# An RWKV block and a gated feed-forward layer: two of seven gate and up products split once more, one block's weight sums kept in SBUF

## The chip, the cores and the metric

The kernel runs on one core of one Trainium2 chip. The metric is the device time of one launch in microseconds; the median of three runs of the kernel before is 1233.91 us (1233.78 to 1234.72). One further execution was taken with the hardware profiler, and the profile below is of that one.

## What is computed

The input is `x`, 2048 tokens by 512 channels, all in float32. `_layernorm` is a plain normalization over channels; `attn` is an RWKV layer at its first position; then a gated feed-forward layer follows.

```python
def attn(x):                       # RWKV time mix and channel mix
    h = layer_norm(x, ln1_g, ln1_b); hh = time_shift(h)
    k = (h * tm_mk + hh * (1 - tm_mk)) @ Wk.T      # v and r likewise
    wkv = ...                                      # elementwise, of k and v
    x = x + sigmoid(r) * wkv @ Wo.T
    h = layer_norm(x, ln2_g, ln2_b); hh = time_shift(h)
    kk = (h * cm_mk + hh * (1 - cm_mk)) @ Wkey.T   # 512 -> 2048
    kv = silu(kk) @ Wval.T                         # 2048 -> 512
    return x + sigmoid((h * cm_mr + hh * (1 - cm_mr)) @ Wcr.T) * kv

def ffn(h):
    gate, up = split(h @ w_gate_up.T, 2)           # 512 -> 2 x 2048
    return (silu(gate) * up) @ w_down.T            # 2048 -> 512

x = x + attn(_layernorm(x))
x = x + ffn(_layernorm(x))
```

## The kernel before

The 2048 tokens are worked in four blocks of 512 (`TB`), numbered 0 to 3 in the code and called block one to four here. Each 512x512 weight is cut into quarters of 256x256, and each product with it is done by Strassen's scheme in Winograd's form: seven products of quarters instead of eight. The operands of these seven are the quarters A11, A12, A22 and B11, B12, B21, B22, and sums of quarters: S1 to S4 of the weight, T1 to T4 of the activation (T3 takes the place of B12). The sums of the activations are made by VectorE in `sums_of`. The weights' sums are made once: `prepare` loads the four quarters of a weight into tiles of the pool `prep` (six tiles), makes S1 to S4 with four VectorE additions, and writes them to DRAM from GpSimd's queue. Afterwards `weight` loads a quarter or a sum, 256 KB, from DRAM into a ring of twelve tiles (`wring`) on SyncE's queue. The down products, 2048 to 512, go one Strassen level deeper on one side, with their own prepared sums (`"d"` and `"dd"`).

One gate or up unit (`unit`) is one 512x512 weight against one block's operand `zT`. Its seven products are `step1` to `step7`; each has four matmul calls of 128x128 against 256 columns. Three of them share PSUM contents: `step1`'s result is copied by ScalarE from the bank `z` into the accumulator `accv`, on which `step2` goes on; after `step5`, `z` is copied into `accx`, on which `step3` goes on. The last three products of a unit (`step7`, `step3`, `step4`) are held and popped between the first products of what comes next. `sink` receives each finished quarter: for a gate, ScalarE's Silu; for an up, VectorE's multiplication with the gate's quarter into the hidden tiles.

The order on TensorE, VectorE and ScalarE is that in which the Python program emits instructions. The program has its own planner. After each product `tick` adds `SHARE` (0.88) times the product's planned time (`STEP`, 1.72 us) to a balance, `slack`, from which the planned cost of VectorE's work is taken. While the balance is positive, `tick` emits work that is not tied to a product: first steps of weight preparation (`prep_one`), each of which needs one `credit`, then a queue of urgent steps (`hot`: sums of operands), then the `background` (norms, mixes). `credit[1]` is what one tick adds to the credit, at most 2.0 are kept, and `pause` is the number of ticks between the loads of a preparation and its first addition. `need` emits all that is left of a named piece of work, whatever the balance says.

The stages at the end are in this order: `ffn_gate(0, 0)`; then for each block b the gate and up units g = 0 to 3, the first gate of block b + 1, and the down products of block b. `ffn_in(b + 1)` is the last norm of the next block: it adds the residual and `x`, takes the moments, forms the reciprocal root with eleven small VectorE steps, scales on VectorE (`scaled`), transposes on TensorE and evacuates with ScalarE. It is pushed to the background in block b after the second up unit; the residual and `x` are loaded by `load_resid`.

The list `late` gives the order of preparations: first those of the value weights, then all eight gate and up weights, then those for the down products. They are worked off in the background from the first attention blocks on, and the last ones while block one's gate and up units run.

PSUM has eight banks: `accv`, `accx` and a pool `ps` of six.

Of the kernel before, what the change touches and what calls it, by code (L numbers as in the profile page):

```python
# [15 lines left out]
P = 128  # L16
# [5 lines left out]
EPS = 1e-5  # L22
WAIT = 5
LONG = 6
STEP = 1.72
SHARE = 0.88
WARM = 24
# [36 lines left out]
def rwkv_ffn_kernel(  # L64
# [20 lines left out]
    up = ctx.enter_context(tc.tile_pool(name="up", bufs=10))  # L85
    prep = ctx.enter_context(tc.tile_pool(name="prep", bufs=6))
    small = ctx.enter_context(tc.tile_pool(name="small", bufs=3))
    ps = ctx.enter_context(tc.tile_pool(name="ps", bufs=6, space=bass.MemoryType.PSUM))
    pv = ctx.enter_context(tc.tile_pool(name="pv", bufs=1, space=bass.MemoryType.PSUM))
    px = ctx.enter_context(tc.tile_pool(name="px", bufs=1, space=bass.MemoryType.PSUM))  # L90
    dram = ctx.enter_context(tc.tile_pool(name="dram", bufs=1, space=bass.MemoryType.DRAM))


# [16 lines left out]
        return tokp.tile([P, NT, H], F32, tag="tok", name=name)  # L110

    def bank():
        return ps.tile([P, 2, HB], F32, tag="ps", name="ps")

# [29 lines left out]
    def value_part(q, k):  # L146

        if q < 4:
            return wv[q, k].rearrange("p (g c) -> p g c", c=P)
        m, kk = divmod((0, 1, 3, 2)[k], 2)  # L150
        return vsum[q - 4][:, :, kk, m * P : (m + 1) * P]

    for q in (A11, A12, A22, S1, S2, S3, S4):
        sources["vv", q] = [value_part(q, k) for k in range(4)]
# [40 lines left out]
    def ring(src):  # L195
        t = wring.tile([P, 2, HB], F32, tag="w", name="w")
        nc.sync.dma_start(flat(t), src)
        return t

    def weight(n, q):  # L200
        if q >= 4:
            need_sums(n)
            return ring(sums[n][q - 4])
        return ring(sources[n][q])

    def down_weight(q, k):

# [10 lines left out]
    def value_weight(q, k):  # L218

        if k >= 4:  # L220
            need_sums(("vv", q))
            return ring(sums["vv", q][k - 4]).rearrange("p a (h c) -> p (a h) c", c=P)
        if q >= 4:
            for g in range(4):
                need_sums(WVAL + g)
        t = wring.tile([P, 2, HB], F32, tag="w", name="w")
        t = t.rearrange("p a (h c) -> p (a h) c", c=P)
        nc.sync.dma_start(t, value_part(q, k))
        return t

    def load_x(b, queues=None):
        t = tok_tile("x")
# [58 lines left out]
    preps = deque()  # L291
    credit = [0.0, 0.0]
    pause = [WAIT]

    def prep_one():
        item = preps[0]
        if item[1] > 0:
            return False
        try:
            if next(item[2]) is not None:  # L300
                item[1] = pause[0]
        except StopIteration:
            preps.popleft()
            finished.add(("sums", item[0]))
            if len(preps) > 1 and item[3] > 1:
                begin(preps[1])
            elif preps:
                begin(preps[0])
        return True
# [7 lines left out]
    def prepare_all(ns, own, depth):  # L317
        empty = not preps
        for n in ns:
            preps.append([n, 0, prepare(n, own), depth, False])  # L320
        if empty:
            for item in list(preps)[:depth]:
                begin(item)
# [58 lines left out]
    nc.vector.memset(warm, 0.0)  # L382
    nc.scalar.activation(warm, warm, AF.Exp)

    pt = ps.tile([P, 2, HB], F32, tag="ps", name="warm")
    for _ in range(WARM):
        nc.tensor.transpose(pt[:, 0, 0:P], ident, ident)

# [41 lines left out]
    def tt(out, a, b, op):  # L430
        nc.vector.tensor_tensor(out, a, b, op)  # L431
        cost(size(out))
# [140 lines left out]
    def release():  # L573
        while held:
            pop_held()
# [7 lines left out]
    def unit(weights, Bs, sink, by_token, done=None, free=None):  # L583
# [86 lines left out]
        for s in order:  # L670
            if s is None:
                pop_held()
            else:
                s()
                tick()
        held.extend(((STEP, step7), (STEP, step3), (STEP, step4)))

    def plain_unit(n, B, sink, by_token, done=None, free=None, halfway=None, hold=False):

# [451 lines left out]
    def ffn_in(b):  # L1131
        r, xr = loads.pop(b)
        for t in range(NT):
            tt(r[:, t, :], r[:, t, :], xr[:, t, :], ALU.add)
            yield
        rs[b] = r
        mv = small.tile([P, NT, 2], F32, tag="mv", name="mv")
        yield from moments(r, mv)
        var = small.tile([P, NT], F32, tag="var", name="var")
        ts(var, mv[:, :, 1], EPS, None, ALU.add)  # L1140
        rstd = small.tile([P, NT], F32, tag="rstd", name="rstd")
        yield from rsqrt(var, rstd, NT)
        z = tok_tile("z")
        yield from scaled(r, z, mv, rstd)
        m, B = op_tile("zT")
        ops[b, "z"] = B
        yield 1

        def evacuate(c, pt):
            k = c // 2  # L1150
            nc.scalar.copy(
                m[:, 2 * k : 2 * k + 2, c % 2, :], pt.rearrange("p (j t) -> p j t", j=2)
            )

        yield from transposed(z, evacuate)
        finished.add((b, "z"))
        yield 1
        yield from sums_of(B)

    gated = {}  # L1160

    def ffn_gate(b, g):
        s = gated[b, g] = {}

        tile_of = q_tile if g % 2 else u_tile

        def sink(i, j, c):
            t = tile_of("s")
            nc.scalar.activation(t, c, AF.Silu)
            s[i, j] = t  # L1170

        unit([WG + g], [Lazy((b, "z"))], sink, False)

    def ffn_up(b, g):
        s = gated.pop((b, g))
        hid = hidden.setdefault(b, {})

        def sink(i, j, c):
            q = (B11, B12, B21, B22)[2 * i + j]
            if q not in hid:  # L1180
                hid[q] = hidden_tile()
            tt(hid[q][:, g], c, s[i, j], ALU.mult)
            if g == 3:
                made.add((b, q))
                if q in (B11, B22):
                    quarter_sums(b, 0 if q == B11 else 1)

        unit(
            [WU + g],
            [Lazy((b, "z"))],  # L1190
            sink,
            False,
            lambda: hidden_done(b, g),
            op_done if g == 3 else None,
        )

    def hidden_done(b, g):
        hid = hidden[b]
# [35 lines left out]

    def last_room():
        middle.close()
        pools["q"] = ctx.enter_context(
            tc.tile_pool(name="fq", bufs=4, reuse_waits="tile")
        )

    def quarters(t):
        return {2 * k + m: t[:, :, k, m * P : (m + 1) * P] for k in range(2) for m in range(2)}
# [212 lines left out]

    early = [WV, WCR, WO] + [WKEY + g for g in range(4)] + [WVAL, WVAL + 1]
    late = [("vv", q) for q in (A11, S4, S2, A12, S1, S3, A22)]
    late += [n + g for g in range(4) for n in (WG, WU)] + [("dd", A11)]
    late += [("d", k) for k in range(4)] + [("dd", q) for q in (S4, S2, A12, S1, S3, A22)]

    ctx.enter_context(
        tc.manual_schedule(
# [25 lines left out]
    for b in range(NB):  # L1488
        nxt = b + 2 < NB
        if nxt:  # L1490
            xin[b + 2] = load_x(b + 2)
        if b == NB - 1:
            load_resid(0)
        if b >= DEEP:
            credit[1], pause[0] = 1.0, LONG
        gate_unit(b)
        if b + 1 < NB:
            out_unit(b + 1)
        if b == DEEP:
            need((b, "ck"))  # L1500
            mixes.close()
            deep_room()
        need((b, "ck"))
        if nxt:
            push(f"norm{b + 2}", time_norm(b + 2))
        for g in range(4):
            up_unit(b, g)
            if b == 1 and g == 0:
                credit[1] = 0.55
            if b == NB - 1 and g == 0:  # L1510
                push((0, "z", "t"), ffn_in(0), op_free)
            if g == 0:
                if nxt:
                    push_mix(b + 2, "k", time_mix(b + 2, "k"))
                    push_residual(b + 2)
                    push_mix(b + 2, "r", time_mix(b + 2, "r"))
                if b + 1 < NB:
                    push(f"normb{b + 1}", channel_norm(b + 1))
                if nxt:
                    push_mix(b + 2, "v", time_mix(b + 2, "v"))  # L1520
                if b + 1 < NB:
                    push_mix(b + 1, "cr", channel_mix(b + 1, "cr"))
                    push_mix(b + 1, "ck", channel_mix(b + 1, "ck"))
        if b == 1:
            credit[1] = 0.8
        if b >= DEEP:
            credit[1] = 0.0
        down_unit(b)
        if nxt:
            for n, u in (("k", k_unit), ("r", r_unit), ("v", v_unit)):  # L1530
                u(b + 2)
    credit[1] = 0.75
    need((0, "z"))
    ffn_gate(0, 0)
    last_room()
    for b in range(NB):
        for g in range(4):
            if g > 0:
                need((b, "z"))
                ffn_gate(b, g)  # L1540
            if g == 0 and b + 1 < NB:
                load_resid(b + 1)
            ffn_up(b, g)
            if g == 1 and b + 1 < NB:
                push((b + 1, "z", "t"), ffn_in(b + 1), op_free)
        if b + 1 < NB:
            need((b + 1, "z"))
            ffn_gate(b + 1, 0)
        ffn_down(b)
    release()  # L1550
    flush()

# [77 lines left out]
```

## Time and profile before

| what | value |
|---|---|
| median of three runs | 1233.91 us |
| the profiled execution | 1231.09 us |
| its span, first to last instruction | 1229.0 us |
| TensorE busy | 1219.5 us, 6860 matmul records |
| VectorE busy | 780.3 us |
| ScalarE busy | 368.4 us |
| GpSimd busy | 186.6 us |
| DMA | 319.03 MB, mean 260 GB/s |
| granted TensorE clock | 1.000 |

Stages of the end, as the timeline shows them (from the span's start): block one's gate and up units from about 655 us to 752, the first gate of block two to 765, block one's down products to 809, then blocks two, three and four in the same way to 1229.

A line of the profile's groups names line, engine, operation, written and read tiles, shapes and count, then busy time and mean duration of one. The chain of waits starts at the last instruction and goes back, at each step to what released it. In the slices, each digit is the busy share of a fortieth of the span in tenths. A matmul call on float32 appears as two records, each with its own weight load. Matmuls overlap, so the spacing of starts, not the duration of one, is what a stream of them costs.

### The profile page before, as it was taken

How to read it: one execution, taken by the hardware profiler on the slowest of the kernel's cores; microseconds unless marked ns; L12 is line 12 of the kernel's file. 1: busy time of each engine (PE TensorE's matmuls, PEld its weight loads, DVE VectorE, ACT ScalarE, POOL GpSimd, SP SyncE). 2: the span in 40 equal slices, each digit the busy share in tenths (PEclk: the TensorE clock that was granted, in tenths of full speed). 3: DMA queues.
4: the chain of work that ended last, by engine and by line, in shares of the span. 5: the costliest groups of instructions: out<-in, count | busy, mean ns of one | idle time of the engine just before them, and what ended most of it. 6: DMA issues, size and time to landing. Idle time of an engine off the chain costs nothing.

```text
span 1229.0 us, 19201 instructions
## 1 busy us (share of the span) xinstructions
PE 1219.5 (99%) x6860; PEld 1106.3 (90%) x6860; DVE 780.3 (63%) x1451; ACT 368.4 (30%) x713; POOL 186.6 (15%) x334
## 2 busy tenths in 40 slices
PE   9999999999999999999999999999999999999998
PEld 8888888888888888998899888998899888998898
DVE  5877686577685666886775577646546364553466
ACT  5534252242532333323412222112221232112211
POOL 2232221223212222002201222200000000000000
PEclk9999999999999999999999999999999999999999
DMA  5768985899888988899889978995469745785576
GB/s 196 250 221 282 319 299 206 302 320 302 277 262 270 312 288 263 261 297 381 280 281 329 335 232 279 362 343 154 146 194 309 258 143 153 250 290 154 153 225 204
DMA packets 159620, 319.03 MB, mean 260 GB/s; under 512 B 19096, under 2 KB 32552, under 8 KB 158248
## 3 DMA queue, kind: packets, MB, share of 16 engines
q1 hardware_dynamic: 132000, 230.22, 58.4%
q0 software_dynamic: 25920, 84.96, 19.0%
q10 hardware_dynamic: 1608, 2.65, 0.7%
q8 instruction: 55, 0.90, 0.3%
q14 instruction: 37, 0.30, 0.1%
HBM read 268.46 MB, written 49.29 MB: 259 GB/s over the span
## 4 chain that ended last, share of the span: by engine, by line
PE 90%; DVE 4%; DMA 3%; ACT 2%; issue 1%; POOL 1%; ACTq 0%; DVEq 0%; POOLq 0%
PE ps L602 45%; PE ps L1342 21%; PE accx L602 9%; PE accv L602 9%; PE ps L704 5%; DMA raw<-in_w 2%; PE ps L487 1%; DMA vsum<-raw 1%; DMA row<-stats 1%; ACT mix L540 1%; DVE raw L431 0%; DVE e L439 0%; DVE h L435 0%; DVE st L445 0%; POOL raw L181 0%
## 5 line engine op out<-in xcount | busy, mean ns | idle before, releaser
L602 PE MATMUL ps<-zT,w 128*128 128x256 f32 x1280 | 289.3, 380 | 0.0
L602 PEld LDWEIGHTS ps<-zT,w 128*128 128x128 f32 x1280 | 242.4, 191 | 31.5
L602 PE MATMUL ps<-mix,w 128*128 128x256 f32 x920 | 211.1, 380 | 1.3 <-ACT u L633 1.3
L602 PEld LDWEIGHTS ps<-mix,w 128*128 128x128 f32 x920 | 174.3, 190 | 24.5 <-ACT u L633 1.7
L1342 PE MATMUL ps<-w,hid 128*128 128x128 f32 x1248 | 156.8, 275 | 0.0
L1342 PEld LDWEIGHTS ps<-w,hid 128*128 128x128 f32 x1248 | 149.7, 192 | 1.2
L1342 PE MATMUL ps<-w,quads 128*128 128x128 f32 x1056 | 133.5, 276 | 0.4 <-ACT r L1354 0.4
L1342 PEld LDWEIGHTS ps<-w,quads 128*128 128x128 f32 x1056 | 126.4, 192 | 1.1 <-ACT r L1354 0.5
L1354 ACT COPY r<-ps 128x128 f32<-128x128 f32 x168 | 44.5, 265 | 204.5 <-PE ps L1342 201.9
L431 DVE TENSOR_TENSOR raw<-raw 128x512 f32<-128x512 f32 x120 | 82.5, 688 | 30.9 <-issue 11.1
L431 DVE TENSOR_TENSOR u<-u,accx 128x512 f32<-128x512 f32 x64 | 43.8, 685 | 85.7 <-ACT accx L637 85.7
L431 DVE TENSOR_TENSOR hid<-hid 128x512 f32<-128x512 f32 x126 | 84.9, 687 | 2.0 <-ACT hid L1068 0.3
L622 ACT COPY accv<-ps 128x512 f32<-128x512 f32 x64 | 36.5, 571 | 158.0 <-PE ps L602 155.2
L637 ACT COPY accx<-ps 128x512 f32<-128x512 f32 x64 | 36.5, 570 | 132.7 <-PE ps L602 126.2
L431 DVE TENSOR_TENSOR u<-ps,u 128x512 f32<-128x512 f32 x64 | 44.2, 690 | 44.5 <-PE ps L602 40.6
L704 PE MATMUL ps<-mix,w 128*128 128x256 f32 x320 | 70.8, 380 | 1.1 <-DVE mix L439 1.1
L633 ACT COPY u<-ps 128x512 f32<-128x512 f32 x64 | 37.4, 584 | 109.5 <-PE ps L602 109.5
L704 PEld LDWEIGHTS ps<-mix,w 128*128 128x128 f32 x320 | 60.4, 191 | 9.5 <-DVE mix L439 1.8
L431 DVE TENSOR_TENSOR r<-ps,r 128x256 f32<-128x256 f32 x83 | 29.8, 359 | 51.5 <-PE ps L1342 47.1
L602 PE MATMUL accv<-zT,w 128*128 128x256 f32 x256 | 60.6, 380 | 0.0
L602 PE MATMUL accx<-zT,w 128*128 128x256 f32 x256 | 60.5, 380 | 0.0
L602 PE MATMUL ps<-w,t 128*128 128x256 f32 x264 | 59.4, 379 | 0.0
(179 smaller groups left out, 1593.7 us busy)
## 6 DMA issues: line engine op xcount, KB each, us to landing
w<-sum SPq DMA_DIRECT2D x248, 256.0 KB, 4.2
w<-in_w SPq DMA_DIRECT2D x230, 256.0 KB, 4.2
w<-dd SPq DMA_DIRECT2D x112, 256.0 KB, 3.8
w<-vsum SPq DMA_DIRECT2D x56, 256.0 KB, 4.4
w<-vv SPq DMA_DIRECT2D x56, 256.0 KB, 4.0
raw<-in_w POOLq DMA_DIRECT2D x48, 256.0 KB, 6.7
w<-d SPq DMA_DIRECT2D x48, 256.0 KB, 3.5
sum<-raw POOLq DMA_DIRECT2D x40, 256.0 KB, 4.1
```

Of the source, the lines that this page charges most:

```text
L431: nc.vector.tensor_tensor(out, a, b, op)
L487: nc.tensor.transpose(flat[:, t * P : (t + 1) * P], h[:, t, c * P : (c + 1) * P], ident)
L540: nc.scalar.activation(dst(c), hT[:, c, 0:TB].rearrange("p (j t) -> p j t", j=2), AF.Copy, scale=onem[:, row - MK, c : c + 1],)
L602: mm = nc.tensor.matmul(pz[:, m, :], lhsT=lhsT, rhs=rhs, start=first and g == 0 and m == 0 and k == 0, stop=g == last and k == 1, skip_gro ...
L622: "z", A11, B11, True, pop_held, read=lambda: nc.scalar.copy(accv, acc["z"])
L633: nc.scalar.copy(tmp["u2"], acc["z"])
L637: nc.scalar.copy(accx, acc["z"])
L704: mm = nc.tensor.matmul(acc[i, j][:, m, :], lhsT=act[:, k, lo] if by_token else wg[:, k, lo], rhs=wg[:, k, :] if by_token else act[:, k, : ...
L1342: mm = nc.tensor.matmul(dst, lhsT=x[k][:, g, :], rhs=wt[:, g, :], start=first and g == 0, stop=g == 3, skip_group_check=True,)
L1354: nc.scalar.copy(st["r"][:, m, n * P : (n + 1) * P], st["z"])
```

## The change

Four things change, and the constants of the planner with them.

1. From the first up unit of block two on, gate and up units are done by `paired_unit`. It makes five products at full size. The two others, A11 with B11 and S3 with T3, are made for both at once by `inner`, one Strassen level deeper: seven products of half size, two calls each against 128 columns. These small steps belong to the next unit and are spread between the full products of the current one. The results lie in SBUF, in halves of one permanent tile (`pair`). A11's result is copied into `z` and `accv` by ScalarE, S3's (`plus`) is added by VectorE when (1, 1) and (1, 0) are formed. The first up unit of block two still makes all seven at full size, since no small steps precede it. One product of a unit is held instead of three.

2. The small products need the small sums of A11 and S3 of each weight (`small_sums`, eight VectorE instructions of 128 columns) and of the activation (`inner_sums`). For seven of the eight gate and up weights the sums are no longer prepared in the background: `jit_load` brings the quarters into the weight ring during block one, `jit_sums` makes S1 to S4 there, block one's units use these tiles directly, and they are written to DRAM for the later blocks. The list `late` loses these seven. All other preparations are emitted before block one's units begin.

3. PSUM is divided anew after block one's down products (`pair_room`, which first emits all held products): `accv`, `accx`, `z`, `w` and four banks of `ps`.

4. `ffn_in` scales on ScalarE, with the shift made from mean and reciprocal root first. It and the loads of its operands are queued earlier.

```diff
 def weight(n, q):
+    if n in jit and (n, q) not in at_once:
+        at_once.add((n, q))
+        while q not in jit[n]:
+            run_one(True)
+        return jit[n][q]
...
+def jit_load(n):
+    jit[n] = {}
+    for q in (A22, A21, A11, A12):
+        t = wring.tile([P, 2, HB], F32, tag="w", name="w")
+        nc.sync.dma_start(t, w[n, q])
+        jit[n][q] = t
+
+def jit_sums(n):
+    x = jit[n]
+    for o, i0, i1, op in ((S1, A21, A22, ALU.add), (S2, S1, A11, ALU.subtract),
+                          (S3, A11, A21, ALU.subtract), (S4, A12, S2, ALU.subtract)):
+        t = x[A21] if o == S3 else prep.tile([P, 2, HB], F32, tag="raw", name="raw")
+        tt(t, x[i0], x[i1], op)
+        x[o] = t
+        nc.gpsimd.dma_start(sums[n][o - S1], flat(t))
+        yield
+    for q in (A11, S3):
+        yield from small_sums(n, q, x[q])
...
 def prep_one():
...
+        item[5] += 1
+        if item[5] == AHEAD[0] and item[3] == 1 and len(preps) > 1:
+            begin(preps[1])
...
+def inner(n, b):                       # the small steps of one unit
+    def one():
+        st["w"] = [weight(n, A11), weight(n, S3)]
+        st["s"] = [inner_weight(n, A11), inner_weight(n, S3)]
+        mm(st["z"], A11, B11, True);  keep(0, 0)     # keep: ScalarE copy to SBUF
+        mm(st["y"][:, :, 0, :], A12, B21, True)
+    def two():    mm(st["z"], S2, T2, False);  keep(1, 0)
+    def three():  mm(st["z"], S1, T1, False);  keep(0, 1);  mm(st["y"][:, :, 1, :], S4, B22, False)
+    def four():   mm(st["z"], S3, "T3", False);  keep(1, 1)
+    def five():   mm(st["z"], A22, T4, False);  tt(r1, st["z"], r1, ALU.add)
...
+def paired_unit(at, b, n, after, sink, done=None, free=None):
+    small(); pop_held()
+    small(); product(z, S2, T2);      nc.scalar.copy(aw, z);    tick(); pop_held()
+    small(); product(accv, A12, B21); sink(0, 0, accv);         tick()
+    small(); product(z, S1, T1);      nc.scalar.copy(accx, z);  sink(1, 1, z, plus);  tick()
+    small(); nc.scalar.copy(z, r);    nc.scalar.copy(accv, r)
+    product(aw, A22, T4);             sink(1, 0, aw, plus);     tick()
+    held.append((STEP, last))         # last: product(accx, S4, B22); sink(0, 1, accx)
...
 def ffn_in(b):
-    yield from scaled(r, z, mv, rstd)
+    stt(shift, mv[:, :, 0], -1.0, rstd, ALU.mult, ALU.mult)
+    for t in range(NT):
+        nc.scalar.activation(z[:, t, :], r[:, t, :], AF.Identity,
+                             bias=shift[:, t : t + 1], scale=rstd[:, t : t + 1])
+        spent[0] += 0.3
+        yield
...
-late += [n + g for g in range(4) for n in (WG, WU)] + [("dd", A11)]
-late += [("d", k) for k in range(4)] + [("dd", q) for q in (S4, S2, A12, S1, S3, A22)]
+late += [WG, ("dd", A11)]
+late += [("d", k) for k in range(4)] + [("dd", q) for q in (A12, S4, S2, S1, S3, A22)]
...
-            credit[1], pause[0] = 1.0, LONG
+            credit[1], pause[0], AHEAD[0] = CREDIT, LONG, 2      # CREDIT = 0.65
...
-    credit[1] = 0.75
     need((0, "z"))
+    while preps:
+        need_sums(preps[-1][0])
     ffn_gate(0, 0)
...
+            if g == 1 and b == 0:
+                push((b + 1, "z", "t"), ffn_in(b + 1), op_free)
-            if g == 0 and b + 1 < NB:
+            if g == 0 and 0 < b < NB - 1:
                 load_resid(b + 1)
             ffn_up(b, g)
+            if g == 0 and b == 0:
+                load_resid(b + 1)
-            if g == 1 and b + 1 < NB:
+            if g == 0 and 0 < b < NB - 1:
                 push((b + 1, "z", "t"), ffn_in(b + 1), op_free)
...
         ffn_down(b)
+        if b == 0:
+            pair_room()
```

## The prediction, made before the result

> **What bounds the kernel now.** First the page's head and its slices: which engine is full, and is its clock whole.
>
> ```profile
> PE 1219.5 (99%) x6860; PEld 1106.3 (90%) x6860; DVE 780.3 (63%) x1451; ACT 368.4 (30%) x713; POOL 186.6 (15%) x334
> ...
> DVE  5877686577685666886775577646546364553466
> ...
> PEclk9999999999999999999999999999999999999999
> ```
>
> TensorE is busy 99% at a full granted clock; no other engine is above 63%. A busy PE row could still hide bad spacing, so next comes the chain that ended last, from 740 us on, where nearly all that the change touches lies.
>
> ```profile
> 770.23 39.30 PE ps L1342 x352
> 826.95 6.91 PE ps L602 x32
> 851.12 6.91 PE ps L602 x32
> ```
>
> The chain is PE instructions end to end. It also prices them: 39.30 / 352 = 0.1117 us for one record with 128 moving columns (down product), 6.91 / 32 = 0.2159 us for one with 256 (gate and up units). A matmul call leaves two records, so a product of four calls is 8 records, 1.73 us. Only products that vanish, or waits that appear, move the end. Third, the windows: block one's gate and up stage, then block two's.
>
> ```profile
> 655.00:752.00 97.00, 97.00 (x467) 85.99 (x466) 58.31 (x105) 25.19 (x45) 21.63 (x41) 1.00 0.87 295
> 809.00:895.00 86.00, 86.00 (x417) 76.33 (x417) 42.58 (x80) 21.70 (x40) 1.43 (x2) 1.00 0.61 191
> ```
>
> After the length the columns are PE, PEld, DVE, ACT, POOL, clock, DMA share, GB/s. DVE has 39 us free of 97 in block one, 43 of 86 in block two; DMA has room too. Last, what a wait costs when nothing lies between a product and the product that needs its copy:
>
> ```profile
> 1221.54 1.95 PE L1342 MATMUL ps<-w,hid 128*128 128x128 f32 x16
> 1223.84 1.16 PE L1342 MATMUL ps<-w,quads 128*128 128x128 f32 x8 [0.35 <-ACT r L1354]
> ```
>
> Sixteen records take 1.79 us, so the next should have started at 1223.33; it started 0.51 us late. That is the price of one product, ScalarE copy, product in a row.
>
> **The gain: two products split.** `paired_unit` does five of a unit's seven products at full size. The other two (A11 with B11, S3 with T3: 16 records of 256 columns) become seven products of half size for both at once in `inner`: 14 calls, 28 records of 128 columns. Before: 16 x 0.2159 = 3.455 us. After: 28 x 0.1117 = 3.126 us. Saved: 0.329 us a unit, since one level of Strassen saves an eighth. Units that get it: the first gate of block two stays `unit`, its up partner does all seven at full size, so 6 units of block two and 8 each of blocks three and four: 22. 22 x 0.329 = 7.2 us. All of it is on the path. The small steps stand between full products, 1.73 us apart, so their copies (0.27 us for 128 columns, 0.57 for 512) have time.
>
> The Trainium skill ("TensorE: Matmul & The Clock Gate", section "Back-to-back issue gap") gives about 81 ns per matmul at 128 columns in a stream of loads and matmuls; by it the saving would be 22 x (3.455 - 28 x 0.081), some 26 us, an estimate. Its section "LDWEIGHTS" speaks against halving columns: a weight load lasts columns of weight / 1.2, 107 ns, however few columns move; by that, an estimate of 10 us. The row's 0.1117 is close to the second, and the row decides.
>
> **What it adds on other engines, blocks two to four.** DVE: two 256-column adds and one of 512 per unit, 2 x 0.425 + 0.69 = 1.5 us; 4 small sums per block. The two accumulator updates of a unit (2 x 0.69) come back as the additions of `plus`. Eight units: +12 us, less 4 x 0.543 of the norm: about 53 of 84 us. ScalarE: four copies of 256 columns (0.27 to 0.57 each) and one of 512 more: about 2.1 us a unit, 40 of 84. Neither fills up. The tightest handoff is the single accumulator `z`: VectorE reads it, then ScalarE reloads it, before the next unit's S2 product. Between lie small step five (0.45), A22 (1.73), small one (0.89), the held S4 (1.73) and small two (0.45): 5.2 us against 0.69 + 0.60 + 0.57 of work. Cover 3.4 us; cost zero; without it the lag beyond 3.4 us per unit. Four `ps` banks in place of six: in the down stages VectorE frees a bank 0.3 to 1.1 us after its product and the next is due 2.7 us later: zero.
>
> SP: nine weight loads of 0.26 MB a unit instead of seven: seven in 12.1 us are 152 of the window's 191 GB/s, so nine make 191 + 2/7 x 152 = about 235, where other slices move up to 381. Four tiles of twelve are kept through a unit; eight still run ahead, about 8 x 1.7 us against 4.2 us to landing: zero. The residual loads move by one unit on the same queue behind loads that are twelve tiles ahead: zero.
>
> **What it adds on the path.** (a) `pair_room` calls `release` after the first down stage: the last two held products run back to back, each waiting for a copy: 2 x 0.51 = 1.0 us. Between 0.5 and 2 with a bank waited for. (b) The norm's scaling goes to ScalarE. The nearest row is a scale and shift there of the same shape (line 788), 803 ns, against 543 on VectorE: 4 x 0.80 = 3.2 us, charged 0.3 each by the planner, so often four in one tick. Queued behind them are the small steps' copies, wanted 1.2 us after a product (1.73 less 0.5). Bounds per block: 0 (spread over ticks) to 2.0 (all four ahead of one copy). With four banks, two held by `inner`, the four transposes and their 0.60 us evacuations may cost 0 to 0.8 more. For two paired blocks 0 to 5.6; I take 1.8, nearer the low end, because the trace shows such evacuations two to a tick and no PE gap. (c) Block one, below: 0.6.
>
> **Block one's weights in place.** Seven matrices leave the background (28 additions, between 388 and 505 us) and are summed inside block one: per unit four sums of 512 (0.69) and eight of 128 (0.294): 5.1 us of VectorE, plus 2.4 for the first. Leaving that window: 21 preparation sums (14.4 us) and four scalings (2.2). 58.3 - 14.4 + 35.5 + 2.4 - 2.2 = 79.6 of 97 us, 82%; the planner hands out up to 88%. Added wait: the fourth sum needs one of six `prep` tiles, and the earliest falls free when the unit's fourth product ends (6.9 us in); the planner reaches it after the second (3.5 us). Queued behind on VectorE: the up sinks and next block's norm. Five units x 3.4 = 17 us idle: 97 of 97. So cover is thin, though PE needs those results only about five products (8 us) later. If block two's norm is late at `need`, PE stands: bounds 0 to 7 (reciprocal root 2.4, four scalings 3.2, lag). I take 0.6, since before ended its norm at 727 us, 25 us early, and the change starts one unit earlier. POOL: six writes a unit at 0.55 = 3.3 us of 12.1, nothing waits.
>
> **Preparations pulled ahead.** All must be emitted before block one. In the third and fourth attention blocks' 77 ticks, 0.65 x 77 = 50 steps are allowed; about nine preparations x 5 = 45 are left. Before did 8.5 there. Short by one: four sums, 2.8 us on VectorE with its loads already landed, hidden by gate (0, 0). Cost 0; two short, up to 9.
>
> **Sum.** 1231.1 (the profiled execution; span 1229.0, 2.1 around it) - 7.2 + 1.0 + 1.8 + 0.6 = 1227.3. The median shown is 2.8 above that execution: 1230.1 us, 3.8 less than 1233.9. With nothing lost the floor is 1226.7. About 0.2% (2.5 us) is what a measurement of this kernel can tell from no change.
>
> **Rivals.** *Given back* (0.22): same mechanism, but (a) to (c) sum to 5 to 9: 1231.7 to 1236. For it: scalings at 0.80 charged 0.3, transposes with two free banks. Against: PE shows no such gap now, with ScalarE 30% busy. *VectorE becomes the bound in block one* (0.18), the slower side: the wait for `prep` tiles on top of 80 us. It decides once idle passes 17 us in the window; then block two's norm and sums end late and gate (1, 0) stands. Price: 3 us of overflow and the 7 of the norm's chain, up to 14 with the sums T1, T2 behind quarter sums: 1230.1 - 0.6 + 7 to 14 = 1237 to 1243. Against: the start one unit earlier. *The ring runs dry* (0.05): if a kept tile's slot is the one the next S4 load waits for, 4.2 - 2.6 = 1.6 us in each of 22 units, +35: about 1265. Against: slots are taken as they fall free. That the split does not happen is excluded by the code.
>
> **How the numbers follow.** Forecast 0.55: 1230.1, its own range 1227.2 to 1231.4. The range goes up into block one's case, to 1239; above it lie the ring and half of that case. Faster by over 0.2%: 0.55; within: the lower rival, 0.22; slower: 0.23.
>
> **What would show it.** Right: 616 records of 128 columns from the small steps at 0.11 each, gate and up units of blocks three and four about 11.8 us instead of 12.1, PE still 99%, VectorE near 80 of 97 in block one. Wrong: PE idle before a small step or before S2 released by ScalarE; a gap of microseconds at the first transposes of block two; PE waiting for `w` tiles.

## The result and the profile after

The changed kernel's median is 1245.99 us (1243.97 to 1250.42), beside 1234.32 (1233.78 to 1235.36) for the kernel before on the same chip: ratio 1.0098, 95% interval 1.007 to 1.0127. It is slower, by 11.7 us, where 3.8 us less were forecast; the time lies above the range, whose end was 1239.0. The profiled execution took 1246.27 us (span 1244.5), so by the two profiles the difference is larger, 15.2 us: the profiled execution of before was 3.2 us below its median here. What follows accounts for the two profiles.

First the head of the page after and its slices.

```profile
PE 1223.4 (98%) x7124; PEld 1110.5 (89%) x7124; DVE 819.9 (66%) x1582; ACT 419.4 (34%) x840; POOL 180.2 (14%) x322
...
PEclk9999999999999999999899999999999999999999
```

TensorE is busy 3.9 us longer than before, though its work is less, and one slice of the granted clock is an 8. Next the chain of waits and the windows that answer to those of before (block one's gate and up stage, then block two's paired units).

```profile
788.23 39.32 PE ps L1704 x352
921.04 1.73 PE accz L881 x8
```
```profile
664.00:761.00 97.00, 91.05 (x409) 78.58 (x408) 65.45 (x159) 22.03 (x39) 23.71 (x44) 0.96 0.71 246
838.00:924.00 86.00, 85.40 (x498) 77.38 (x497) 55.54 (x106) 36.82 (x77) 0.00 (x0) 1.00 0.65 207
```

The prices are as before: 39.32 / 352 is 0.1117 us, 1.73 / 8 is 0.216. In the window of paired units TensorE is busy 85.4 of 86 us. The first window holds a loss: 91.05 of 97 at a clock of 0.96. Cutting both traces at the first record of each down (or value) product gives the account:

| from ... to the first record of | before | after | of the difference |
|---|---|---|---|
| span's start, attention block four's value product | 607.8 | 614.5 | +6.7 |
| block one's down product | 154.4 | 165.7 | +11.3 |
| block two's down product | 142.3 | 149.4 | +7.1 |
| block three's | 142.3 | 141.6 | -0.7 |
| block four's | 128.5 | 123.0 | -5.5 |
| the last record of all | 49.5 | 46.0 | -3.5 |

The last four rows come to -2.6 (two held products, 3.45 us, have moved from the last row to block two's): the split, less new stops. The first two rows, +18.0, are the loss. The spacing of matmul starts beyond the nominal (0.2159 us after a record of 256 columns, 0.1117 after one of 128) shows where it falls: 15.6 us are lost between 550 and 700 us, where before lost 0.1.

**The stop at 591 us.** TensorE, ahead of block one's first unit, transposes that block's normalized input:

```profile
591.29 0.33 PE L567 MATMUL ps<-ident,z 128*128 128x128 f32 x1
593.45 0.47 PE L567 MATMUL ps<-ident,z 128*128 128x128 f32 x1 [1.83 <-ACT z L1418]
594.15 0.48 PE L567 MATMUL ps<-ident,z 128*128 128x128 f32 x1 [0.22 <-ACT z L1418]
```

TensorE waits here for the scaling on ScalarE (line 1418), started late because VectorE came late to the norm. VectorE's lines of that time, then GpSimd's queue (idle time ahead and its releaser in brackets):

```profile
569.51 2.14 DVE L511 TENSOR_TENSOR raw<-raw 128x512 f32<-128x512 f32 x3 [9.12 <-issue]
...
583.43 0.69 DVE L511 TENSOR_TENSOR raw<-raw 128x512 f32<-128x512 f32 x1 [5.17 <-DMA raw<-d]
```
```profile
559.68 0.54 POOL L190 DMA_DIRECT2D raw<-d  x1 [4.31 <-DVE x L519]
560.60 0.54 POOL L190 DMA_DIRECT2D raw<-d  x1 [0.38 <-DMA dd<-raw]
561.13 1.08 POOL L201 DMA_DIRECT2D dd<-raw  x2
```

With `AHEAD`, the next preparation's four loads are issued while the running one still holds four of the six `prep` tiles. The last two loads go out 5 and 6 us after the first two. For the second of them the trace names one of the running preparation's writes (`dd<-raw`); for the first it names VectorE, with another of those writes landed 0.5 us before. The remaining writes stand behind those loads on GpSimd's queue. The loads are late, the planner's next additions come at their set time all the same, and VectorE, which takes its work in order, stands 9.1 and 5.2 us with the norm behind them. For the first wait the page names nothing, but the load issued at 560.60 landed at 569.43, 0.08 us before VectorE went on. In the kernel before, the waits ahead of such additions, at 561 and 577 us, are 2.1 and 2.4 us.

**The stops at 669 and 681 us.** TensorE stops 2.11 and 3.45 us for weights (`w<-sum`):

```profile
670.79 7.10 PE L682 MATMUL ps<-zT,w 128*128 128x256 f32 x24 [1.95 <-DMA w<-sum]
684.64 2.79 PE L682 MATMUL accx<-zT,w 128*128 128x256 f32 x8 [3.29 <-DMA w<-sum]
```

SyncE's queue, in the order of issue:

```profile
660.09 4.73 SPq L266 DMA_DIRECT2D w<-in_w  x4
666.26 2.05 SPq L206 DMA_DIRECT2D w<-sum  x2
668.88 8.15 SPq L266 DMA_DIRECT2D w<-in_w  x4
...
679.65 0.33 SPq L206 DMA_DIRECT2D w<-sum  x1
```

Line 266 is `jit_load`. It takes four ring tiles at a time for quarters needed one or two units later; the sums that TensorE wants next are behind them, and each waits for a tile to come free.

**The clock.** Windows of the changed kernel, from the stretch ahead of each fall of the granted clock:

```profile
590.10:593.50 3.40, 1.48 (x8) 0.82 (x6) 2.88 (x6) 3.08 (x6) 2.14 (x4) 1.00 1.02 311
593.50:600.30 6.80, 6.35 (x22) 5.23 (x23) 1.39 (x2) 4.13 (x7) 1.08 (x2) 0.50 0.60 227
668.60:672.00 3.40, 1.45 (x9) 1.16 (x8) 1.88 (x8) 0.00 (x0) 0.54 (x1) 1.00 0.91 320
672.00:675.40 3.40, 3.40 (x10) 2.65 (x9) 1.34 (x5) 0.57 (x1) 0.19 (x1) 0.50 0.36 100
682.20:685.60 3.40, 0.96 (x5) 0.89 (x6) 2.14 (x8) 0.00 (x0) 2.01 (x4) 1.00 0.98 383
```

After each of these stops the clock is 0.50 for 3.4 or 6.8 us, 13.7 us in all. The count of a window takes in records that reach into it; in the one from 672.00 on, eight start, 0.427 us apart, where sixteen would at the full clock. Of the 15.6 us lost, the stops themselves are 9.0 (at 591, 2.05 + 0.59 + 0.59 + 0.25; then 2.11 + 3.45); the other 6.6 are nearly all the halved clock.

### The profile page after: what moved, and what is told of

Same layout as the page of the kernel before. It is cut to its first block, busy times and chain, and to the rows that moved or that the text cites. A ratio compares the mean times of both kernels' runs of the same rounds, so it can differ in the third digit from the quotient of the medians.

```text
span 1244.5 us, 20022 instructions
## 1 busy us (share of the span) xinstructions
PE 1223.4 (98%) x7124; PEld 1110.5 (89%) x7124; DVE 819.9 (66%) x1582; ACT 419.4 (34%) x840; POOL 180.2 (14%) x322
## 4 chain that ended last, share of the span: by engine, by line
PE 84%; DMA 5%; DVE 5%; ACT 3%; issue 2%; POOL 1%; DVEq 0%; POOLq 0%; ACTq 0%
PE ps L682 26%; PE ps L1704 21%; PE accz L881 6%; PE accx L682 5%; PE ps L798 5%; PE accv L682 5%; PE ps L975 4%; PE accv L881 3%; PE accx L881 3%; PE accw L881 3%; PE ps L567 1%; DMA raw<-in_w 1%; DMA raw<-d 1%; DMA w<-sum 1%; DVE raw L511 1%
## 5 line engine op out<-in xcount | busy, mean ns | idle before, releaser
L511 DVE TENSOR_TENSOR raw<-raw 128x512 f32<-128x512 f32 x92 | 63.1, 686 | 48.2 <-issue 18.7
L881 PE MATMUL accz<-zT,w 128*128 128x256 f32 x376 | 89.0, 380 | 0.0
L881 PEld LDWEIGHTS accz<-zT,w 128*128 128x128 f32 x376 | 68.0, 190 | 7.4
L511 DVE TENSOR_TENSOR r<-r 128x128 f32<-128x128 f32 (+1 forms) x83 | 40.2, 486 | 36.3 <-ACT r L1716 34.9
L1800 POOL DMA_DIRECT2D out<-resid x12 | 8.6, 715 | 362.5 <-DVE resid L511 336.9
L682 PE MATMUL ps<-zT,w 128*128 128x256 f32 x248 | 58.1, 388 | 2.7 <-DMA w<-sum 1.9
L511 DVE TENSOR_TENSOR quads<-hid,quads 128x512 f32<-128x512 f32 x84 | 57.7, 686 | 1.4
L798 PEld LDWEIGHTS ps<-inner,w 128*128 128x128 f32 x352 | 52.4, 191 | 6.1 <-ACT pair L809 1.5
L682 PEld LDWEIGHTS ps<-zT,w 128*128 128x128 f32 x248 | 47.7, 195 | 10.2 <-issue 2.1
L702 ACT COPY accv<-ps 128x512 f32<-128x512 f32 x41 | 23.4, 572 | 97.7 <-PE ps L682 94.9
```

Source lines behind the costliest of these rows:

```text
L682: mm = nc.tensor.matmul(pz[:, m, :], lhsT=lhsT, rhs=rhs, start=first and g == 0 and m == 0 and k == 0, stop=g == last and k == 1, skip_gro ...
L702: "z", A11, B11, True, pop_held, read=lambda: nc.scalar.copy(accv, acc["z"])
L798: m = nc.tensor.matmul(dst[:, i, :], lhsT=wt(i, q), rhs=act(i, k), start=start and i == 0, stop=True, skip_group_check=True,)
L881: mm = nc.tensor.matmul(dst[:, m, :], lhsT=wg[:, kk, m * P : (m + 1) * P], rhs=act[:, kk, :], start=start and m == 0 and kk == 0, stop=kk ...
L1800: eng.dma_start(out_t[b][:, tokens, cols], rs[b][:, tokens, cols])
```

## The experiments

Times are against runs of the kernel before on the same chip. "Loss" is spacing of matmul starts beyond nominal in the profiled execution. The ratios of the first two experiments lie inside the changed kernel's interval (1.007 to 1.0127), so their times alone show no gain; what they show is in their traces.

**Scaling back on VectorE.**

```diff
-        stt(shift, mv[:, :, 0], -1.0, rstd, ALU.mult, ALU.mult)
-        for t in range(NT):                       # ScalarE, line 1418
-            nc.scalar.activation(z[:, t, :], r[:, t, :], AF.Identity, ...)
+        yield from scaled(r, z, mv, rstd)
```

> The changed kernel with one part undone: the last norm is scaled on VectorE again. Theory A (a late norm behind VectorE's wait for a preparation's loads): the norm of block one still stands behind 9.1 and 5.2 us of waiting for raw tiles, so TensorE still stands at its transposes near 591 us, a little less since four scalings on VectorE take 2.0 us and not 3.2; 0 to 2 us faster than the changed kernel, 1244 to 1246. Rival B (the scaling on ScalarE alone causes that stop): the stop and the halved clock behind it go, 6 us faster, about 1240.

Ratio 1.0091 (1.0073 to 1.0109), span 1241.1. VectorE still waits 7.9 and 5.3 us for the preparation, yet the loss from 550 to 600 us is 0.8 instead of 6.2, and the clock there stays whole. The scaling on ScalarE was needed for the stop, as the rival had it. The ring's stops stay (2.26 and 3.97).

**Preparations paced as before.**

```diff
-            credit[1], pause[0], AHEAD[0] = CREDIT, LONG, 2
+            credit[1], pause[0] = 1.0, LONG
```

> The changed kernel with the planner's old constants in the third and fourth attention blocks (one credit a tick, no early loads for the next preparation). Theory A: VectorE no longer waits 5 to 9 us for raw tiles, the norm of block one is on time, the stop near 591 us and the halved clock go: 6 us faster than the changed kernel, about 1240, although the scaling stays on ScalarE. Rival B: the stop stays, 1246. Both: at most one unfinished preparation is emitted ahead of block one, 0 to 3 us.

Ratio 1.0079 (1.0058 to 1.0099), span 1239.7. The loss there is 0.09 us with the scaling still on ScalarE. TensorE's timeline of this run at the same transposes has no wait:

```profile
593.21 1.47 PE L567 MATMUL ps<-ident,z 128*128 128x128 f32 x12
...
596.25 0.60 PE L567 MATMUL ps<-ident,z 128*128 128x128 f32 x4
```

So the stop needed both, a late VectorE and a scaling in four slow steps behind ScalarE's other work; either alone is nearly hidden. The ring's stops are still there, 1.44 and 4.08 us.

**Block one's loads put off.**

```diff
-                later(lambda: jit_load(m), 5 if at == 0 else 4)
+                later(lambda: jit_load(m), 6 if at == 0 else 7)
```

> The changed kernel with the loads of the third and fourth weights of block one emitted later (after six products in place of five, after seven in place of four). Theory A (loads for the next units take all twelve ring tiles and stand ahead of the first gate's last weights on the queue): the two waits for weights near 669 and 681 us (2.1 and 3.5 us) and the halved clock behind them (3.0) go, 7 to 9 us faster than the changed kernel, 1237 to 1239. Rival C (VectorE is the bound in block one): no change, or a new wait for the later sums, 1245 to 1250.

Ratio 1.0044 (1.0029 to 1.0058), span 1233.9. The stops for weights are gone, the clock is not halved between the first products and the last, and block one's row of the account falls from 165.7 to 158.1. The same two groups of records now start without a wait:

```profile
665.15 5.40 PE L682 MATMUL ps<-zT,w 128*128 128x256 f32 x24
...
673.83 1.89 PE L682 MATMUL accx<-zT,w 128*128 128x256 f32 x8
```

This was the larger cause. At 591 us TensorE still stands for ScalarE, but 2.0 us (0.83 + 0.59 + 0.59) instead of 3.5; nothing of this edit lies ahead of that point, so the size of that stop varies by run, and with it whether the clock falls. Two stops of 1.4 and 1.2 us remain in block one, at 689 and 694 us. The first waits for VectorE, the second for a ScalarE copy that itself waits for VectorE.

**No split.** All gate and up units at full size; the small sums of the weights are still made but not used, those of the activations are not made.

```diff
-        if b == 0 or (b, g) == (1, 0):
+        if True:                                  # in ffn_gate and ffn_up: unit
...
-        if b == 0:
-            pair_room()
```

> The changed kernel without the split: all gate and up units of blocks two to four do seven full products from six banks, everything else stays, the small sums of weights too (nothing reads them). Theory A: the split saves 7.2 us on TensorE and gives back about 4.5 in blocks two to four (1.0 where all held products are released, the rest in waits under 1 us), so this runs 2 to 4 us slower than the changed kernel, 1248 to 1250. Rival D (the small steps cost more than they save): this is faster than the changed kernel.

Ratio 1.0134 (1.0118 to 1.015), span 1247.0. The same stops stand at 591, 668 and 680 us, so the split is not their cause; the last four rows of the account are 142.7, 142.7, 128.5 and 49.5, within 0.4 us of those of before. Beside the changed kernel's 1.0098 the split is worth 0.0036 of 1234 us, 4.4 us, but the two intervals overlap. The rows say 3.4 (463.4 less 460.0), beside the 7.2 of the sum: what the split saves less the stops that it brings.

**Early loads taken out alone**, the credit left at 0.65.

```diff
-            credit[1], pause[0], AHEAD[0] = CREDIT, LONG, 2
+            credit[1], pause[0] = CREDIT, LONG
```

> The changed kernel with the early loads of preparations taken out alone; the credit per tick stays at 0.65. Theory: it is the early loads, which sit in the six tiles that the running preparation needs, that make VectorE wait 9 and 5 us between 560 and 590 us; without them VectorE waits there under 1 us at a time, and the stop of 3.8 us at the first transposes near 591 us goes. With fewer steps done in time, some additions are left over for the place ahead of block one's first gate, where they may cost up to 3 us. Rival: the credit of 0.65 with its long pause makes the norm late; then the stop near 591 us stays.

One run of 1258.92 us, where before has 1231.81; span 1257.2. The stop at 591 us is gone (loss 0.09), so it was the early loads that made it. But the leftover cost far more than the 3 us expected. VectorE, then TensorE, of this run:

```profile
665.70 2.87 DVE L511 TENSOR_TENSOR raw<-raw 128x512 f32<-128x512 f32 x4 [7.82 <-issue]
675.03 2.87 DVE L511 TENSOR_TENSOR raw<-raw 128x512 f32<-128x512 f32 x4 [6.45 <-DMA raw<-in_wd]
```
```profile
680.01 3.78 PE L682 MATMUL ps<-zT,raw 128*128 128x256 f32 x8 [4.09 <-DVE raw L511]
690.19 3.75 PE L682 MATMUL accx<-zT,w 128*128 128x256 f32 x8 [6.41 <-DVE pair L511]
```

Two preparations were left; emitted ahead of gate (0, 0) they put load, wait and additions on VectorE twice, with block one's sums behind them. The loss from 650 to 750 us is 26.1 us, where the changed kernel loses 10.3; the clock is at a half for 23.9 of these 100 us. At credit 0.65 the early loads were the lesser evil; at 1.0 they are not needed.

**Both causes taken away.** The edits of the second and third run together, and then with the scaling on VectorE as well.

> The changed kernel with the preparations paced as before (credit 1.0, no early loads) and the three late loads of block one's weights put off by one and three more products. Theory: the two causes add, and each stop costs its own length plus about half of the time in which the clock is halved after it. Then block one loses under 4 us between 550 and 750 us instead of 16, no product runs at half clock, the span is 1228 to 1231 and the ratio to the kernel before 0.998 to 1.002. Rival: the delays only move, to the norm of block two or to the next weights; then the ratio stays at 1.004, as with the put-off loads alone.

> As the run before it, with the norm's scaling back on VectorE as well. Theory: with the norm on time the scaling hides on either engine; within 1 us of the run with it on ScalarE, ratio 0.998 to 1.002. Rival: the scaling on ScalarE is itself a cost in blocks two to four (1.8 us in the prediction); then this one is 1.5 to 2.5 us shorter, ratio 0.996 to 0.999.

Ratios 1.0026 (1.0017 to 1.0035) and 1.0013 (1.0003 to 1.0023), spans 1232.1 and 1231.3. The losses between 550 and 750 us are 3.5 and 3.4 us and the clock stays whole, so the two causes do add; the first ratio is a little above what was expected. The intervals overlap: what the place of the scaling costs with the norm on time, if anything, isn't settled by the times. In both traces the transposes of blocks three and four stand 0.40 us each, so there its place makes no difference.

**The small sums' slots.** In the first of these two, VectorE still waits in block one, and TensorE behind it:

```profile
676.93 0.29 DVE L511 TENSOR_TENSOR pair<-w 128x128 f32<-128x128 f32 x1 [2.26 <-DMA in<-pair]
...
687.06 0.29 DVE L511 TENSOR_TENSOR pair<-w 128x128 f32<-128x128 f32 x1 [6.99 <-DMA in<-pair]
```
```profile
688.74 3.72 PE L682 MATMUL ps<-zT,w 128*128 128x256 f32 x16 [1.06 <-DVE hid L511]
693.45 1.99 PE L682 MATMUL ps<-zT,w 128*128 128x256 f32 x8 [0.99 <-ACT accx L717]
```

The second of TensorE's stops names a ScalarE copy that had itself waited for VectorE. VectorE's releaser is the write of a slot of the permanent tile `pair` to DRAM. The first gate weight's small sums, made during its unit, share slots 2 and 3 with the second gate weight's.

```diff
-        k = (n < WU) * 2 + (q == S3)
+        k = (WG < n < WU) * 2 + (q == S3)
```

> The kernel with preparations paced as before and the loads put off, with one index changed: the small sums of the first gate weight go into the slots 0 and 1 of the permanent tile instead of 2 and 3, which the second gate weight's small sums use at the same time. Theory: VectorE's waits of 2.3 and 7.0 us for the DMA that writes a slot to DRAM, at 674 and 680 us, go, and with them the two stops of TensorE of 1.2 us at 687 and 692 us; span 1229.5 to 1230.5, 2.4 us less than without the edit, ratio 1.0002 to 1.0012. Rival: VectorE waits there for the weights' loads or for the six preparation tiles behind it; then the stops stay, and the ratio at 1.0026.

Ratio 1.001 (1.0 to 1.002), span 1230.4. TensorE's two stops are gone, with one index:

```profile
688.24 5.34 PE L682 MATMUL ps<-zT,w 128*128 128x256 f32 x24
693.42 1.89 PE L682 MATMUL accv<-zT,w 128*128 128x256 f32 x8
```

**The place of the new PSUM division.**

```diff
+        if b == 0:
+            pair_room()
         ffn_down(b)
-        if b == 0:
-            pair_room()
```

> The preparations paced as before, the loads put off, and the new division of PSUM placed ahead of block one's down products instead of behind them, so that the held products that it emits are a unit's last three, none of which waits for a copy. Theory: the two stops of 0.52 us near 827 us go and nothing comes in their place: 1 us shorter than the same kernel without the move, ratio 0.997 to 1.001. Rival: the new banks wait for the old ones, so that the first down products stand for a bank: 1 to 2 us longer.

Ratio 1.0019 (1.001 to 1.0028), span 1232.2, against 1.0026 without the move. The two stops of 0.52 us went, but the first down product stood 1.02 us for a bank that VectorE still read: theory and rival both, and nothing gained.

**Stops put in by hand.** The kernel before, with extra ScalarE copies and a transpose that waits for them; nothing else changed.

```diff
             product("z", A11, B11, True, pop_held, read=...)
+            if stop[0]:                           # 1 to 6, in six up units
+                t = u_tile("stop"); nc.scalar.copy(t, acc["z"])
+                for _ in range(stop[0]): nc.scalar.copy(t, t)
+                nc.tensor.transpose(bank()[:, 0, :P], t[:, 0, :P], ident)
+                stop[0] = 0
```

> The kernel before, with six stops of TensorE put in by hand, one in the first product of six up units of blocks two to four: 2 to 7 ScalarE copies of 512 columns in a row, and then one transpose that has to wait for them (about 1.5, 2, 2.6, 3.2, 3.7 and 4.3 us). Theory: a stop above some length, between 2 and 3.5 us by the stops seen, is followed by 3.4 or 6.8 us at half the granted clock, so the span grows by the stops, 17 us, and by about 1.7 us for each 3.4 us at half clock, 22 to 28 us in all. Rival: the halved clock in the changed kernel was not the stops' doing; then the clock stays at 1.00 throughout and the span grows by 17 us alone.

One run of 1260.6 us, span 1258.6: 29.6 us more by the spans of the two profiles. The stops were 2.03, 2.68, 3.33, 3.98, 4.63 and 5.28 us, 21.9 in all where 17 were meant. After the last three the clock fell to a half, for 6.8, 6.8 and 3.4 us; after the first three it did not. Around those three falls the loss exceeds the stops by 6.6 us. Windows of this run: two stretches with no fall behind them, then one with it:

```profile
830.70:834.10 3.40, 1.64 (x8) 1.11 (x6) 3.30 (x6) 1.64 (x3) 0.00 (x0) 1.00 0.55 159
...
980.90:984.30 3.40, 1.44 (x7) 1.31 (x8) 1.17 (x2) 1.84 (x3) 0.00 (x0) 1.00 0.20 64
...
1032.10:1035.50 3.40, 1.19 (x6) 0.71 (x4) 3.30 (x6) 2.06 (x4) 0.00 (x0) 1.00 0.56 157
1035.50:1042.30 6.80, 5.19 (x13) 4.21 (x14) 0.18 (x1) 2.09 (x4) 0.00 (x0) 0.50 0.05 4
```

**All mendings together**: the paces, the loads, the slots, the scaling on VectorE, and the PSUM division ahead of the down products with the four shared banks placed first (`for n, bufs in (("ps", 4), ("z", 1), ("w", 1))`), so that the bank in use isn't the next one wanted.

> All mendings together: preparations paced as before, loads put off, the slots changed, the norm's scaling on VectorE, the new division of PSUM ahead of block one's down products and its four shared banks placed first. Theory: what is left over the kernel before is the 7.2 us saved less about 3 us of single stops of 0.4 to 1.0 us in blocks two to four and less 1 to 2 us elsewhere: span 1226 to 1228.5, ratio 0.998 to 1.000. Rival: the stops come back elsewhere, since the program emits the same work; then 1.001, as without the last two mendings.

1230.65 us against 1231.81, ratio 0.999 (0.9981 to 0.9999), span 1227.6. The granted clock stays whole:

```profile
PEclk9999999999999999999999999999999999999999
```

No stop at the change of banks is left. This version beats the changed kernel clearly. It is 0.1% ahead of the kernel before, which is at the limit of what these runs can tell: the interval ends at 0.9999.

## Why the prediction was wrong

**The gain held.** The small steps are 352 + 264 = 616 records, as counted. In block four seven units have lost their two products and six have small steps in them: 7 x 3.455 - 168 x 0.1117 = 5.4 us, and that row of the account, which has no new stop, is 5.5 us shorter. A unit saves 9.5% of these two products and not the eighth that the prediction names, since a record of 128 columns takes 0.1117 us, more than half of 0.2159. By the 81 ns per matmul of 128 columns of the Trainium skill ("TensorE: Matmul & The Clock Gate", section "Back-to-back issue gap") an estimate would have been 24.2 - 168 x 0.081 = 10.6. The row of the trace was the right price. The rest of the 7.2 us went as the other rows show.

**The failed steps.** Two costs taken at zero were not.

- *Preparations pulled ahead: "Cost 0".* The step counted whether there were ticks enough for 45 steps. It did not follow the DMAs that the earlier start issues: eight tiles wanted where there are six, loads that wait on GpSimd's queue for the writes of the preparation before, and a VectorE that stands in order behind them. With the scaling on ScalarE, which was costed for two paired blocks and not for block one's own norm, it cost 3.5 us of stop and a halved clock. The run without early loads shows the step's other side, "two short, up to 9": two were short, and in the one run block one lost 15.8 us more than in the changed kernel.
- *SP's ring.* The step counted weight loads in blocks two to four. Block one's `jit_load`, 28 loads on the same queue, was never put there, though the diff has it on `nc.sync` and the ring has twelve tiles. This was the larger one, 5.6 us of stops. The rival *The ring runs dry* had the mechanism with a chance of 0.05, but in the paired units and over a kept tile.

The halved clock, 6.6 us of the loss, was in no case: every stop was priced at its length.

**The other terms.** (a), `release`, was right: two stops of 0.52 us, at 827.26 and 828.77. (b), 1.8 for the scaling and the four banks, is in blocks two and three 0.4 + 0.4 us (transposes that wait for an evacuation); they stay when the scaling goes back to VectorE. (c): block two's transposes lose 1.0 us, beside 0.6. *VectorE becomes the bound in block one* failed: VectorE is busy 65.5 of 97 us, and 74.7 in the best run, where the stops do not stretch the stage; block two's norm was not late by microseconds. The sum of 79.6 added up durations, 0.294 us for a small sum, while those in a row start 0.24 us apart. That rival's price, 7 to 14 us, leaves its own 3 us of overflow out of its lower end. VectorE's wait for slots of `pair`, 7 us in one run, was not foreseen; the step had looked at the `prep` tiles alone. Not in the sum: the small step behind a unit's last product, 0.52 twice, and the S4 product in block three, 0.8 to 1.6 us late in these runs. In the runs with the split this product starts 0.13 to 0.14 us after a weight (`w<-sum`) has landed, in the changed kernel at 986.65 us, 6.5 us after its issue. So the sign "PE waiting for `w` tiles" came in the paired units too, but once and not in each; why that load is late was not tested. All stops from the first down product on come to 4.6 us beyond those of before: even with block one's causes mended, only about 2.6 of the 7.2 us would be left, and the best run kept 1.2 by its median.

## What to carry to other kernels

A load moved earlier costs at two places that a count of busy time doesn't show: the ring tiles that it holds, and the queue entries that now stand behind it; write down the queue's order with each tile's release before taking it at zero. Work that an in-order engine does "in the background" carries its DMA waits to whatever stands behind it. On TensorE, price a stop of 2 us or more at its length and then at the halved clock that may follow.

## What the runs showed of the hardware

The granted clock changes only at points a multiple of 3.41 us apart (593.5, 600.3, 672.0, 675.4, 685.6, 689.1 in the changed kernel: 6.8 is two such steps, 71.7 is 21), and what decides, as far as these runs show, is how busy TensorE was in the stretch before. Stretches with 0.96, 1.19, 1.45 and 1.48 us busy of 3.40 were followed by half clock, and in the run without the split one with 1.61. Those with 1.44 and 1.64 in the run with stops were not, nor one with 1.62 in the first experiment. So the border lies somewhere about 1.4 to 1.6 us and isn't sharp by these records. A stop of 2.11 us that fell into one stretch was followed by half clock, while one of 3.33 us, spread over two, was not. The Trainium skill ("TensorE: Matmul & The Clock Gate", section "HAM oscillation — how this bites in real kernels") gives the rule that there be no idle gaps over about 3.4 us; these runs show falls after stops of 2.1 us, and the measurement decides.
